# Nested Strassen products: a third one in the output projection, two in theta/phi, and an earlier sum in the last image

## The chip, the cores and the metric

The kernel runs on one core of a Trainium2 chip. The metric is the device time of one execution in microseconds (us); all times here are in that unit unless ns is written. The core has TensorE (matmuls, PE in the profile; its weight loads are PEld), VectorE (DVE), ScalarE (ACT), GpSimd (POOL) and SyncE (SP, which here issues most DMAs). They run their own instruction streams and meet at semaphores. Matmul results land in PSUM, everything else is in SBUF or, for what does not fit, in DRAM.

## The reference

The input x is 8 images of 512 channels and 1024 positions, in float32. For each image a self-attention layer with 8 heads of 64 channels is computed, and then a non-local block on its result:

```python
q, k, v = conv1x1(x, Wq, bq), conv1x1(x, Wk, bk), conv1x1(x, Wv, bv)
attn = softmax(einsum('bhdn,bhdm->bhnm', q, k) * scale)
out = einsum('bhnm,bhdm->bhdn', attn, v)
x1 = x + conv1x1(out, Wp, bp)                 # p

g, theta, phi = conv1x1(x1, g_w), conv1x1(x1, theta_w), conv1x1(x1, phi_w)   # 512 -> 256 channels, each with a bias
f = einsum('bcn,bdn->bcd', theta, phi) / n    # 256 x 256, no softmax
z = conv1x1(einsum('bcd,bdn->bcn', f, g), W_w, W_b) + x1
out = batch_norm(z over all images and positions) * gamma + beta
```

The batch norm needs all eight z, so the last step of the kernel goes over everything again.

## The kernel before, in words

**Images and stages.** The loop at the end of `unshifted` goes over the images b = 0 to 7. For each: attention of image b (scores L578, weighted sums L604), then q, v and k of image b + 1 (`six`), then p of image b (`project`, tile pp), theta and phi together (`theta_phi`, tile ptp, result tp), then `nonlocal_`: g (pg), f (pf), the product wf of f and W_w, and z (pz). In images 5 to 7 z is put off to the end (`late`). f of image 6 and the rest of its non-local block are computed in and after the last attention (`make_f`, two steps of scores after that attention's begin). In the last image p runs in a place of its own: the products of the attention's result o with the reciprocal denominators (`normalize`) run on DVE in four parts, two for each group of rows of o, and p comes right behind; in the images before it they run on GpSimd beside v.

**Seven products.** A projection is a product of a weight matrix with a data matrix. Both are cut into 2 x 2 blocks (quarters 11, 12, 21, 22) and multiplied with seven products in place of eight (Winograd's form of Strassen's scheme): `SEVEN` at L271 lists them with the weight block (0 to 6), the data block (11, 21, 22 or a difference t1 to t4), the PSUM slot and the quarters of the result that read the slot when the product is done. t1 = 12 − 11, t2 = 22 − t1, t3 = 22 − 12, t4 = 21 − t2 (`more_sums`). A slot is a double bank of PSUM; products that are listed with one slot add up in it, so the first matmul of the later one comes after DVE's reads of the earlier one. Weight blocks 3 to 6 are sums of the others (`weight_sums`); most are computed once, in image 0, and kept in DRAM (`keep`).

**Nested products.** A product of two blocks can itself be done with seven products of half the size. In q, k and v six of the seven are (L418, L421). In p of images 1 to 6, `FIVE` products are plain and products 1 and 2 are nested:

```python
FIVE = (SEVEN[0], SEVEN[1], SEVEN[2], SEVEN[3], ("s3t3", 5, "t3", 0, (("22", False), ("21", False))))
STEPS = [0] * 4 + [1] * 14
```

so the slots of the five run 0, 1, 0, 1, 0, and after the first four matmuls one inner matmul (a "step") follows each plain one, in slots of its own (`nested`, tiles pp_in_s at L299). Each step's PSUM result is read by DVE at once into a part of x (`first`, with the bias, or `add`). The inner products need the inner sums of their weight block (four 128 x 128 tiles that are kept beside the block, `extra`) and of their data block (`inner_sums`). Theta/phi is `SEVEN` with no nesting in every image.

**What sets the order.** Instructions given to `pe`, `dve` or `sp` keep the order of the program on their engine (`keep_in_program_order`); the others are placed by a scheduler between them. GpSimd runs, in the time of k, the sums t1 to t4 of o, the inner sums of its blocks 21 and t4, and additions into k.

**Weights.** `plan` lists the matrices in the order of use, `UNITS` into which loads each is cut. A unit goes into a ring of four buffers (`wr`), block 0 ("first") into one of two (`wf0`). `load_w()` issues the next unit on SyncE's queue, at fixed places of the program. A unit of two blocks has room for the inner sums behind each block. For theta/phi the two units are (3, 4, 2) and (6, 5, 1); for p they are (1, 2), (3, 4, 5) and (6). In the last image SyncE's queue also carries sixteen reloads of 512 KB (L918) between the loads of p's and theta/phi's weights, then the biases of theta and phi (L752), the second unit for theta/phi and WgT, and four reloads more (L925).

## Time and profile before

| | us |
|---|---|
| median of 3 runs | 2117.56 (2117.47 to 2119.9) |
| profiled execution | 2118.56 |
| its span | 2116.7 |
| TensorE busy | 2090.3 (99%) |
| VectorE busy | 1403.2 (66%) |
| ScalarE busy | 790.3 (37%) |
| GpSimd busy | 525.9 (25%) |
| p of image 1 (first to last matmul) | 515.44 to 538.65 |
| theta/phi of image 1 | 538.65 to 562.83 |
| p of the last image | 1980.28 to 2011.46 |

How to read it: the busy shares say which engine fills the span. The waits say what an engine stood still for: the total, how often, and the longest. The chain of waits follows the end of the execution back through whatever released each step; where an engine is never idle, the chain is that engine's own work. A timeline lists instructions in order with start and duration, and in brackets the idle time in front of them and what ended it. A matmul in float32 shows as two records; a plain one of p has 512 columns, an inner one 256. One of theta/phi has 256 columns, an inner one after the change 128.

### The profile page before, as it was taken

To read this page: it belongs to the slowest core of one execution; us is meant where nothing else is said; L and a number is where in the kernel's file an instruction comes from. 1 tells how busy PE (TensorE), PEld (TensorE's weight loads), DVE (VectorE), ACT (ScalarE), POOL (GpSimd) and SP (SyncE) were. 2 spreads that over 40 slices of the span, in tenths; PEclk is the share of its full clock that TensorE was granted. 3 is DMA by queue.
4 is the path that set the end of the run, shared out by engine and by line. 5 is a ranking of instruction groups with operands and counts; after the bars stand their busy time and mean duration, and the time that the engine had idled before them with its cause. 6 is when DMAs were issued, how large, how long until landed. Compare 5 with 4: busy or idle time off the path is not lost.

```text
span 2116.7 us, 33247 instructions
## 1 busy us (share of the span) xinstructions
PE 2090.3 (99%) x13486; PEld 1172.5 (55%) x13486; DVE 1403.2 (66%) x2051; ACT 790.3 (37%) x1045; POOL 525.9 (25%) x392
## 2 busy tenths in 40 slices
PE   9999999999999999999999999999999999999996
PEld 4535863357733677337763377633875348733362
DVE  5587567765578655786557766677565775567636
ACT  1464204642046410564106631166303653066016
POOL 0012900138001370014601155011640119011000
PEclk9999999999999999999999999999999999999998
DMA  6253533244232532425314253133544235222758
GB/s 229 83 148 76 174 147 111 40 92 141 100 117 40 120 110 98 120 40 141 122 62 125 40 152 121 72 101 41 170 139 140 39 63 169 75 31 40 268 188 319
DMA packets 71728, 243.56 MB, mean 115 GB/s; under 512 B 12688, under 2 KB 21136, under 8 KB 69520
## 3 DMA queue, kind: packets, MB, share of 16 engines
q1 hardware_dynamic: 60640, 215.01, 30.4%
q0 software_dynamic: 9072, 24.78, 9.5%
q8 instruction: 108, 1.77, 0.3%
q10 hardware_dynamic: 1856, 1.56, 0.3%
q14 instruction: 52, 0.43, 0.1%
HBM read 160.45 MB, written 47.32 MB: 98 GB/s over the span
## 4 chain that ended last, share of the span: by engine, by line
PE 97%; DVE 1%; ACT 1%; DMA 1%; issue 0%; SPq 0%; DVEq 0%
PE ps L578 21%; PE po L604 21%; PE ptp L342 9%; PE pp L342 7%; PE pv_in L418 6%; PE pq_in L421 6%; PE pk_in L421 6%; PE pg L342 4%; PE pz L342 3%; PE pf L801 2%; PE pp_in_s L299 2%; PE pq L388 1%; PE pq L342 1%; PE pv L385 1%; PE pv L342 1%; PE pk L388 1%
## 5 line engine op out<-in xcount | busy, mean ns | idle before, releaser
L581 ACT ACTIVATE e<-ps 128x1024 f32<-128x1024 f32 x512 | 523.0, 1025 | 422.9 <-PE ps L578 412.2
L587 DVE TENSOR_TENSOR acc<-acc,e 128x1024 f32<-128x1024 f32 x384 | 469.9, 1224 | 103.1 <-ACT e L581 92.9
L578 PE MATMUL ps<-q,k 64*64 64x512 f32 x4096 | 529.3, 589 | 0.0
L604 PE MATMUL po<-e,v 64*64 64x512 f32 x4096 | 528.6, 589 | 0.0
L617 POOL DMA_DIRECT2D fold<-acc x189 | 144.8, 766 | 1358.3 <-PE ps L578 690.6
L604 PEld LDWEIGHTS po<-e,v 64*64 64x64 f32 x4096 | 156.6, 133 | 282.9 <-issue 275.5
L578 PEld LDWEIGHTS ps<-q,k 64*64 64x64 f32 x4096 | 155.5, 133 | 283.5 <-issue 277.3
L844 ACT ACTIVATE g<-pg,gb 128x512 f32<-128x512 f32 x31 | 21.3, 688 | 447.0 <-PE pg L342 446.9
L585 DVE TENSOR_TENSOR acc<-e,e 128x1024 f32<-128x1024 f32 x64 | 78.3, 1224 | 121.2 <-ACT e L581 119.0
L342 PE MATMUL ptp<-w_tp,t_x 128*128 128x256 f32 x512 | 114.4, 379 | 0.0
L342 PE MATMUL pp<-t_o,w_WpT 128*128 128x512 f32 x208 | 103.4, 605 | 4.6 <-DVE t_o L252 4.6
L342 PEld LDWEIGHTS ptp<-w_tp,t_x 128*128 128x128 f32 x512 | 97.3, 190 | 13.2
L342 PE MATMUL ptp<-w_tp,x 128*128 128x256 f32 x384 | 86.8, 379 | 0.0
L342 PEld LDWEIGHTS ptp<-w_tp,x 128*128 128x128 f32 x384 | 73.0, 190 | 13.3 <-issue 3.8
L429 DVE TENSOR_TENSOR v<-v,pv_in 128x256 f32<-128x256 f32 x112 | 46.3, 421 | 43.8 <-PE pv_in L418 37.3
L429 DVE TENSOR_TENSOR k<-k,pk_in 128x256 f32<-128x256 f32 x112 | 46.8, 421 | 39.4 <-PE pk_in L421 35.0
L342 PE MATMUL pp<-o,w_WpT 128*128 128x512 f32 x144 | 67.7, 592 | 0.0
L427 ACT COPY v<-pv_in 128x256 f32<-128x256 f32 x84 | 31.4, 374 | 95.8 <-DVE T_pv L429 25.5
L427 ACT COPY k<-pk_in 128x256 f32<-128x256 f32 x84 | 31.3, 373 | 91.6 <-PE pk_in L421 89.9
L684 POOL TENSOR_TENSOR o<-o,r 128x1024 f32<-128x1024 f32 x28 | 65.3, 2372 | 0.0
L772 DVE TENSOR_TENSOR tp<-tp,ptp 128x1024 f32<-128x1024 f32 x24 | 29.3, 1221 | 51.2 <-PE ptp L342 51.2
L737 DVE SCALAR_TENSOR_TENSOR x<-pp,bp,x 128x512 f32<-128x512 f32 x52 | 37.6, 746 | 38.5 <-PE pp L342 38.5
(230 smaller groups left out, 2954.8 us busy)
## 6 DMA issues: line engine op xcount, KB each, us to landing
fold<-acc POOLq DMA_DIRECT2D x189, 128.0 KB, 3.1
w_WqT<-kept_WqT SPq DMA_DIRECT2D x21, 896.0 KB, 4.9
w_WvT<-kept_WvT SPq DMA_DIRECT2D x21, 896.0 KB, 5.0
w_WkT<-kept_WkT SPq DMA_DIRECT2D x21, 896.0 KB, 6.2
r<-den_d SPq DMA_DIRECT2D x32, 512.0 KB, 6.8
x<-in_x_dram SPq DMA_DIRECT2D x30, 512.0 KB, 5.9
spill<-x SPq DMA_DIRECT2D x24, 512.0 KB, 4.0
z<-spill SPq DMA_DIRECT2D x24, 512.0 KB, 9.9
```

The source lines that it names most:

```text
L342: pe(nc.tensor.matmul(to_ps, lhsT(k), rhs(k), start=(s, at) not in begun, stop=(k == nk - 1), skip_group_check=True))
L418: pe(nc.tensor.matmul(ps[:, i, :], d[:, i * P:(i + 1) * P], a, start=start and not i, stop=True, skip_group_check=True))
L421: pe(nc.tensor.matmul(ps, a, d, start=start, stop=True, skip_group_check=True))
L427: nc.scalar.copy(piece(q, i, j), ps)
L429: dve(nc.vector.tensor_tensor(piece(q, i, j), piece(q, i, j), ps, ALU.add))
L578: pe(nc.tensor.matmul(ps[c * P // 2:(c + 1) * P // 2, j, :], k[r, p, keys], q[r, p, h * 512:(h + 1) * 512], start=True, stop=True, skip_gr ...
L581: nc.scalar.activation(e, ps, AF.Exp, scale=SCALE)
L585: nc.vector.tensor_tensor(accs[u], es[u, 0], e, ALU.add)
L587: ins = nc.vector.tensor_tensor(accs[u], accs[u], e, ALU.add)
L604: pe(nc.tensor.matmul(ps[j * D:(j + 1) * D, r, :], v[keys, m, (2 * p + j) * D:(2 * p + j + 1) * D], e[keys, j, :], start=(m == 0), stop=(m ...
L617: nc.gpsimd.dma_start(to, part_of, accum_op=ALU.add)
L684: dve((engine or nc.vector).tensor_tensor(at, at, of, ALU.mult))
```

## The change

Four things are edited together.

- **p, images 1 to 6:** block 6 (quarter 22 of o) is nested as well. The list `FOUR` has the plain products 11, s1t1, s2t2 and s3t3 in slots 0, 1, 0, 0; s1t1 is now read for quarters 22 and 12, and s4 is gone from the list. Inner steps come two after each plain matmul from the fifth to the fourteenth, and one after the fifteenth. The inner sums of block 22 of o are added to GpSimd's work beside k. p's adds are pinned on DVE, and t1 and t2 of x1, the data of theta/phi, are now emitted around the add into quarter 22.
- **Theta/phi, images 1 to 7:** five plain products and two nested ones, 2 and then 1; the fourteen steps begin after the third plain product. t4 of x1 and the inner sums of t4 and of block 21 are on GpSimd. An inner result here has positions on the partitions, so one step is two matmuls of 128 columns. The sums of theta for f are emitted after the last plain product. All first reads and adds of theta/phi are pinned on DVE.
- **Weights:** theta/phi's units become (1, 2), (3, 4, 5), (6), so three loads in place of two; p's unit (6,) gets room for inner sums. In image 0 the inner sums of the newly nested weights are computed on DVE (`nest`) and kept; in this image the load of WgT is issued behind the keeping of p's blocks.
- **Last image:** t1 of o is emitted between the products of o for the first group of rows and those for the second, t2 behind the last one.

```diff
-             "WpT": ((1, 2), (3, 4, 5), (6,)), "tp": ((3, 4, 2), (6, 5, 1)),
+             "WpT": ((1, 2), (3, 4, 5), (6,)), "tp": ((1, 2), (3, 4, 5), (6,)),
...
+        def roomy(self, n):
+            return len(self.blocks(n)) == 2 or self.name == "WpT" and self.blocks(n) == (6,)
...
-    STEPS = [0] * 4 + [1] * 14
+    FOUR = (SEVEN[0], ("s1t1", 3, "t1", 1, (("22", True), ("12", True))), ("s2t2", 4, "t2", 0, (("12", False),)),
+            FIVE[4])
+
+    INNER = {"p": (FOUR, ((1, "21", "11", False), (2, "t4", "21", True), (6, "22", "12", False)),
+                   [0] * 4 + [2] * 10 + [1]),
+             "tp": (FIVE, ((2, "t4", "21", True), (1, "21", "11", False)), [0] * 24 + [1] * 14)}
...
+                if positions_out:
+                    ps = ps.rearrange("p (i f) -> p i f", f=P)
+                    for i in range(2):
+                        pe(nc.tensor.matmul(ps[:, i, :], d[di][:, i * P:(i + 1) * P], a[wi], start=start and not i,
+                                            stop=True, skip_group_check=True))
...
+        nest = 0 < b < B - 1
+        plain_add = add_to(xt, dve if nest else lambda ins: None)
+
+        def add(q, ps):
+            if nest and q == "22":
+                more_sums(x1, (1,), dve)
+            plain_add(q, ps)
+            if nest and q == "22":
+                more_sums(x1, (2,), dve)
...
+        def sums():
+            if "t3" not in data:
+                for i in (4,) if b else (3, 4):
+                    more_sums(data, (i,), dve, nc.gpsimd if b else None)
+            if b:
+                for of in ("t4", "21"):
+                    inner_sums(data, of, dve, nc.gpsimd)
+
+        def third_sum():
+            if "t3" not in data:
+                more_sums(data, (3,), dve)
...
-                more = [lambda of=of: inner_sums(nxt["o"], of, dve, nc.gpsimd) for of in ("21", "t4")]
+                more = [lambda of=of: inner_sums(nxt["o"], of, dve, nc.gpsimd) for of in ("21", "t4", "22")]
...
-            for one in normalize(nxt["d"]):
+            nxt["o"] = data_sums(quarters_of(o), f"o_{b}", ())
+            for n, one in enumerate(normalize(nxt["d"])):
                 one()
+                if n % 2:
+                    more_sums(nxt["o"], (n // 2 + 1,), dve)
+            between[1] = lambda: more_sums(nxt["o"], (3, 4), dve)
...
+        if b == 0:
+            between = {4: lambda: nest(w, 6)}
...
         if b == 0:
             w_p = w
+            kept["WpT"] = dict(kept["plain"])
+            keep("WpT", w_p, (2,))
...
-        between = {} if last else {5: lambda: b < B - 2 and of_theta.append(f_sums(b, tps[0], 0))}
+        between = {} if last else {4 if b else 5: lambda: b < B - 2 and of_theta.append(f_sums(b, tps[0], 0))}
...
         tp = theta_phi(b, w, data, tpb, between)
         if b == 0:
-            keep("tp", w)
-            kept["WpT"] = dict(kept["plain"])
             keep("WpT", w_p, (0,))
             load_w()
+            keep("tp", w, ("first", 1, 2))
+            for i in (1, 2):
+                nest(w, i)
+            keep("tp", w, (0,))
         load_w("first")
-        load_w(times=2)
+        load_w(times=3)
```

More of the change, by code (lines that the diff above doesn't have):

```diff
@@ L116, in unshifted @@
     PAIRS = ((1, 6), (3, 4), (5, 2))
-    UNITS = {"WqT": PAIRS, "WkT": PAIRS, "WvT": PAIRS, "WpT": ((1, 2), (3, 4, 5), (6,)), "tp": ((3, 4, 2), (6, 5, 1)),
+    UNITS = {"WqT": PAIRS, "WkT": PAIRS, "WvT": PAIRS, "WpT": ((1, 2), (3, 4, 5), (6,)), "tp": ((1, 2), (3, 4, 5), (6,)),
              "WgT": (range(7),)}
     WIDTH = 14 * P
-    INNER = (1, 2)
     class Weights:
@@ L131, in __getitem__, with blocks @@
             return self.at[at[1]][(slice(None), *at[2:])]
+        def blocks(self, n):
+            return (0,) if n == "first" else UNITS[self.name][n]
+        def roomy(self, n):
+            return len(self.blocks(n)) == 2 or self.name == "WpT" and self.blocks(n) == (6,)
         def place(self, n, t):
             size, to = 2 * self.half, 0
-            blocks = (0,) if n == "first" else UNITS[self.name][n]
+            blocks = self.blocks(n)
             for i in blocks:
@@ L138, in place @@
                 to += size
-                if n != "first" and len(blocks) == 2:
+                if self.roomy(n):
                     self.extra[i] = t[:, to:to + 3 * P].rearrange("p (i f) -> p i f", i=3)
@@ L146, in whole @@
             t = self.tiles[n]
-            if n == "first" or len(UNITS[self.name][n]) != 2:
+            if not self.roomy(n):
                 return t
-            return t.rearrange("p (b f) -> p b f", b=2)[:, :, :2 * self.half]
+            return t.rearrange("p (b f) -> p b f", b=len(self.blocks(n)))[:, :, :2 * self.half]
         def inner(self, i):
@@ L208, in inner_weights, with nest @@
                                      (s4, a12, s2, ALU.subtract))]
+    def nest(w, i):
+        for one in inner_weights(w, i):
+            one()
     def keep_inner(w):
@@ L282, in unshifted, with nested @@
     FIVE = (SEVEN[0], SEVEN[1], SEVEN[2], SEVEN[3], ("s3t3", 5, "t3", 0, (("22", False), ("21", False))))
-    STEPS = [0] * 4 + [1] * 14
-    def nested(name, w, data, tags, first, add):
+    FOUR = (SEVEN[0], ("s1t1", 3, "t1", 1, (("22", True), ("12", True))), ("s2t2", 4, "t2", 0, (("12", False),)),
[3 more added lines that the diff above has]
+             "tp": (FIVE, ((2, "t4", "21", True), (1, "21", "11", False)), [0] * 24 + [1] * 14)}
+    def nested(name, w, data, tags, first, add, goes_to, positions_out):
         slots = [bank(tag, f"{name}_in_{tag}") for tag in tags]
-        goes_to = {1: ("11", "21", False), 2: ("21", "t4", True)}
-        for n, (q, di, begins) in enumerate(goes_to[i] for i in INNER):
-            a, d = w.inner(INNER[n]), data[f"inner {di}"]
+        for n, (outer, of, q, begins) in enumerate(goes_to):
+            a, d = w.inner(outer), data[f"inner {of}"]
             pair = slots[::-1] if n % 2 else slots
@@ L298, in nested @@
                 ps = pair[s % 2 if s < 2 else 1][:, s // 2, n % 2 * 256:(n % 2 + 1) * 256]
-                pe(nc.tensor.matmul(ps, a[wi], d[di], start=s not in begun, stop=True, skip_group_check=True))
+                start = s not in begun
                 begun.add(s)
-                for to, is_first in reads:
-                    c = rows(q).start + int(to[0]) - 1
-                    at = cols(q).start + (int(to[1]) - 1) * 256
-                    (first if is_first and begins else add)((slice(c, c + 1), slice(at, at + 256)), ps)
+                if positions_out:
[3 more added lines that the diff above has]
+                                            stop=True, skip_group_check=True))
+                else:
+                    pe(nc.tensor.matmul(ps, a[wi], d[di], start=start, stop=True, skip_group_check=True))
+                for to, is_first in reads:
+                    i, j = int(to[0]) - 1, int(to[1]) - 1
+                    if positions_out:
+                        to = q, i, j
+                    else:
+                        c, at = rows(q).start + i, cols(q).start + j * 256
+                        to = slice(c, c + 1), slice(at, at + 256)
+                    (first if is_first and begins else add)(to, ps)
                 yield
     def seven(name, w, data, positions_out, first, add, between=None, early=False,
-              by_chunk=False, inner=False):
+              by_chunk=False, inner=None):
         nk, half = w.shape[2], w.shape[3]
@@ L315, in seven @@
         slots, begun = {}, set()
-        steps, counts = iter(()), iter(STEPS if inner else ())
+        steps, counts = iter(()), iter(())
         if inner:
             free[:] = [tags[1], tags[2], tags[3], tags[0]]
-            steps = nested(name, w, data, tags[2:], first, add)
+            products, goes_to, counts = INNER[inner]
+            counts = iter(counts)
+            steps = nested(name, w, data, tags[2:], first, add, goes_to, positions_out)
+        else:
+            products = LATER if early == "later" else EARLY if early else SEVEN
         def read(reads, ps):
@@ L323, in read @@
                 (first if is_first else add)(to, ps)
-        products = FIVE if inner else LATER if early == "later" else EARLY if early else SEVEN
         for n, (what, wi, di, s, reads) in enumerate(products):
@@ L728, in attention, with project @@
         return o["o"], all_denominators, normalize
-    def project(b, xt, o, w, between, data=None):
+    def project(b, xt, w, between, data, x1):
         def first(q, ps):
@@ L739, in first @@
                     dve(ins)
-        if not data:
-            data = data_sums(quarters_of(o), f"o_{b}", (1, 2), pin=dve)
-            between = {**between, 1: lambda: more_sums(data, (3, 4), dve)}
-        seven(f"pp_{b}", w, data, False, first, add_to(xt), between, early=b == B - 1 and "later", inner=0 < b < B - 1)
+        nest = 0 < b < B - 1
[6 more added lines that the diff above has]
+                more_sums(x1, (2,), dve)
+        seven(f"pp_{b}", w, data, False, first, add, between, early=b == B - 1 and "later", inner="p" if nest else None)
     tps = []
@@ L759, in at, with as_tp, add @@
         def at(q):
+            if isinstance(q, tuple):
+                q, i, j = q
+                m, c = (int(q[1]) - 1) * NB // 2 + j * NB // 4, (int(q[0]) - 1) * CI + i * P
+                return tp[:, m:m + NB // 4, c:c + P]
             return tp[:, (int(q[1]) - 1) * NB // 2:int(q[1]) * NB // 2, (int(q[0]) - 1) * CI:int(q[0]) * CI]
-        def as_tp(ps):
-            return ps.rearrange("p h (i f) -> p (h i) f", f=CI)
+        def as_tp(q, ps):
+            return ps if isinstance(q, tuple) else ps.rearrange("p h (i f) -> p (h i) f", f=CI)
         def first(q, ps):
-            ins = nc.vector.tensor_tensor(at(q), as_tp(ps), tpb[:, int(q[0]) - 1].to_broadcast([P, NB // 2, CI]),
-                                          ALU.add)
-            if q == "11":
-                dve(ins)
-        seven(f"ptp_{b}", w, data, True, first,
-              lambda q, ps: nc.vector.tensor_tensor(at(q), at(q), as_tp(ps), ALU.add),
-              {0: lambda: "t3" in data or more_sums(data, (3, 4), pin=dve), **between})
+            to, of = at(q), tpb[:, int((q[0] if isinstance(q, tuple) else q)[0]) - 1]
+            if isinstance(q, tuple):
+                of = of[:, :, q[1] * P:(q[1] + 1) * P]
+            ins = nc.vector.tensor_tensor(to, as_tp(q, ps), of.to_broadcast(list(to.shape)), ALU.add)
+            if q == "11" or b:
+                dve(ins)
+        def add(q, ps):
+            ins = nc.vector.tensor_tensor(at(q), at(q), as_tp(q, ps), ALU.add)
+            if b:
+                dve(ins)
+        def sums():
+            if "t3" not in data:
+                for i in (4,) if b else (3, 4):
+                    more_sums(data, (i,), dve, nc.gpsimd if b else None)
+            if b:
+                for of in ("t4", "21"):
[3 more added lines that the diff above has]
+                more_sums(data, (3,), dve)
+        seven(f"ptp_{b}", w, data, True, first, add, {0: sums, **({1: third_sum} if b else {}), **between}, inner="tp" if b else None)
         return tp
@@ L1087, in unshifted @@
         w = weights("WpT", sums_done=True)
-        project(b, xt, o, w, between, nxt.get("o"))
+        if b == 0:
+            between = {4: lambda: nest(w, 6)}
+        x1 = data_sums(quarters_of(xt), f"x1_{b}", ())
+        project(b, xt, w, between, nxt["o"], x1)
         if b == 0:
             w_p = w
+            kept["WpT"] = dict(kept["plain"])
+            keep("WpT", w_p, (2,))
         load_w("first")
@@ L1095, in unshifted @@
                 nc.sync.dma_start(spill[b][:, cc, :], xt[:, cc, :])
-        data = data_sums(quarters_of(xt), f"x1_{b}", (1, 2, 3, 4) if last else (1, 2))
+        data = x1
+        if last or not b:
+            more_sums(data, (1, 2, 3, 4) if last else (1, 2))
         if last:
@@ L1102, in unshifted @@
         w = weights("tp")
-        between = {} if last else {5: lambda: b < B - 2 and of_theta.append(f_sums(b, tps[0], 0))}
+        between = {} if last else {4 if b else 5: lambda: b < B - 2 and of_theta.append(f_sums(b, tps[0], 0))}
         if b == 0:
             weight_sums(w, corner["tp"], (3, 4, 5), dve)
-            def nest_p(i):
-                for one in inner_weights(w_p, i):
-                    one()
-            between.update({1: lambda: weight_sums(w, corner["tp"], (6,), dve), 2: lambda: nest_p(1), 3: lambda: nest_p(2)})
+            between.update({1: lambda: weight_sums(w, corner["tp"], (6,), dve), 2: lambda: nest(w_p, 1),
+                            3: lambda: nest(w_p, 2)})
         tp = theta_phi(b, w, data, tpb, between)
         if b == 0:
-            keep("tp", w)
-            kept["WpT"] = dict(kept["plain"])
             keep("WpT", w_p, (0,))
             load_w()
+            keep("tp", w, ("first", 1, 2))
+            for i in (1, 2):
+                nest(w, i)
+            keep("tp", w, (0,))
         load_w("first")
-        load_w(times=2)
+        load_w(times=3)
         def before_wf():
```

## The prediction

> **What bounds the kernel now.** I read the busy shares first, then TensorE's waits, then the chain of waits in one image, then the engines' timelines at the two places that the diff touches. All times are in us.

> ```profile
> PE 2090.3 (99%) x13486; PEld 1172.5 (55%) x13486; DVE 1403.2 (66%) x2051; ACT 790.3 (37%) x1045; POOL 525.9 (25%) x392
> ```
> TensorE is busy for the whole span, so a microsecond of matmul saved counts in full, and so does one of new waiting. DVE has a third of the span free, GpSimd three quarters.

> ```profile
> PE count L1152 <- DVE good L1150: 8.5, 1, 8.5
> PE pp L342 <- DVE t_o L252: 4.6, 1, 4.6
> ```
> TensorE waits twice in all for longer than 1.1: at the very end, and once in the last image's p. Nothing else can be won by removing a wait.

> ```profile
> 515.44 4.29 PE pp L342 x10
> 519.73 0.43 PE pp_in_s L299 x2
> 520.17 0.86 PE pp L342 x2
> ...
> 538.65 24.17 PE ptp L342 x112
> ```
> This is the chain in image 1, in start and duration (two records are one fp32 matmul). p runs 515.44 to 538.65: 20 plain matmuls of 0.858 and 14 inner ones of 0.432, 23.2, with no gap. tp is 7 products of 3.453.

> ```profile
> 729.80 3.45 PE pv L385 x16
> 733.26 18.76 PE pv_in L418 x168
> ```
> v shows the inner form that tp is to get: 168 records in 18.76 are 0.1117 each.

> ```profile
> 528.80 0.75 DVE L737 SCALAR_TENSOR_TENSOR x<-pp,bp,x 128x512 f32<-128x512 f32 x1 [0.44 <-PE pp L342]
> 529.47 0.48 DVE L737 SCALAR_TENSOR_TENSOR x<-pp_in_s,bp,x 128x256 f32<-128x256 f32 x1
> 533.10 0.42 DVE L448 TENSOR_TENSOR x<-x,pp_in_s 128x256 f32<-128x256 f32 x1 [0.81 <-PE pp_in_s L299]
> 533.96 1.22 DVE L448 TENSOR_TENSOR x<-x,pp 128x1024 f32<-128x1024 f32 x1 [0.44 <-PE pp L342]
> 538.69 2.35 DVE L448 TENSOR_TENSOR x<-x,pp 128x1024 f32<-128x1024 f32 x2 [1.23 <-PE pp L342]
> ```
> These are DVE's reads of PSUM in p: 0.42 for an inner result, 1.22 for a whole product, 0.75 (pitch 0.67) for each half of a first read. A read begins 0.04 after TensorE's end (538.65 to 538.69).

> ```profile
> 1980.28 3.60 PE L342 MATMUL pp<-o,w_WpT 128*128 128x512 f32 x8
> 1988.47 5.99 PE L342 MATMUL pp<-t_o,w_WpT 128*128 128x512 f32 x8 [4.59 <-DVE t_o L252]
> ```
> ```profile
> 1977.60 2.36 DVE L684 TENSOR_TENSOR o<-o,r 128x1024 f32<-128x1024 f32 x2 [3.29 <-DMA r<-den_d]
> 1984.92 2.36 DVE L684 TENSOR_TENSOR o<-o,r 128x1024 f32<-128x1024 f32 x2 [4.96 <-DMA r<-den_d]
> 1987.20 1.22 DVE L252 TENSOR_TENSOR t_o<-o 128x1024 f32<-128x1024 f32 x1
> ```
> In the last image p's second product needs t1, which stands behind four products of o, the last two waiting for a transfer. t1 itself needs only the first two, done by 1979.96.

> ```profile
> 1985.00:1990.00 5.00, 1.53 (x2) 0.83 (x3) 4.97 (x5) 0.00 (x0) 0.00 (x0) 0.63 1.02 394
> 1990.00:1995.00 5.00, 5.00 (x9) 2.05 (x8) 1.50 (x3) 0.00 (x0) 0.00 (x0) 0.69 1.02 404
> 1995.00:2000.00 5.00, 5.00 (x13) 2.22 (x12) 4.30 (x5) 0.00 (x0) 0.00 (x0) 1.00 1.03 415
> ```
> The three last columns are granted clock, DMA share and GB/s. That idle time also cost clock: 0.63 and 0.69, then 1.00. Six products after it took 2011.46 − 1988.47 = 22.99 instead of 6 × 3.434 = 20.60, so 2.4. And DMA is saturated here at about 410 GB/s by sixteen reloads of z.

> ```profile
> 2004.91 0.33 SPq L163 DMA_DIRECT2D w_tp<-kept_tp  x1
> ```
> ```profile
> w_tp<-kept_tp SPq DMA_DIRECT2D x1, 768.0 KB, 9.0
> ```
> SyncE issues the second unit of tp's weights behind those reloads at 2004.91, and it lands 9.0 later, at 2013.9.

> **The change, part by part** (the sum stands on the profiled execution of 2118.56, 1.0 above the median of 2117.56).

> *1. Third nested product in p, images 1 to 6.* A plain product of 4 × 0.858 = 3.43 becomes 7 × 0.432 = 3.02: −0.41 × 6 = **−2.5**. p without waits is then 22.8.

> *2. New waits in p, images 1 to 6.* Two of them.
> First, s3t3 accumulates in the slot that s2t2 just left. Before, s4 in the other slot and its inner steps lay between them (over 5 us). Now only inner steps 15 and 16 do (0.86), and DVE must read those two before the add of s2t2 into quarter 12, as the changed order has it. From the end of step 16: 0.04, its read 0.42, 0.03 because the add updates the same quarter (dependent DVE pairs at 302.33 and 303.05 stand 0.72 apart at 0.69 each), the add 1.22, and 0.05 until TensorE starts (1988.42 to 1988.47 above): 1.8. Bounds: with neither inner read ahead of it, 0.04 + 1.22 + 0.05 − 0.86 = 0.45; with one more first read of 0.75 in front, 2.55. I take 1.8, since every term is a row.
> Second, s1t1 is now read twice, for 22 and for 12: four half reads instead of two. From s1t1's end DVE does one (0.67), the inner reads of steps 7 and 8 (0.34, 0.40), three more (2.01), then step 9's (0.48), for which step 11 waits: 3.9 and about 0.1 of hand-over, while TensorE has 3.44 of work until then. 0.6; bounds 0 and 0.9.
> 2.4 × 6 = **+14.4** (0.45 × 6 = 2.7 to 3.45 × 6 = 20.7).

> [...]

> *3. tp's two nested products, images 1 to 7.* A plain one is 3.453, 28 records of 0.1117 are 3.13: −0.33 each, −0.65 an image; images 1 to 6 give **−3.9** (bound 0, if weight loading showed between shorter records; v's 168 show none). The cover: t4 and eight inner sums on GpSimd, one of 2.36 and eight of 0.73 by its rows at 498.38 and 507.77, start some 4.4 after p's end and give the first inner operand at about 7.5; it is needed 11.6 after p's end, after three plain products. If GpSimd took twice as long the spare 4 would be gone. DVE's inner reads (0.42 each, one per 0.87) fit beside the plain ones. Also at nothing: the inner sums of 22 of o (4 × 0.73) delay k's additions on GpSimd (513.50) by 2.9, read only in the next attention; t1 and t2 of x1 now stand around p's last adds on DVE, ready 1.7 and 3.3 after p's end against 3.5 and 6.9; theta's sums start after tp's end, so theta's and phi's (2 × 2.55) end about 7.7 after it, while f starts at 8.58 (562.83 to 571.41): 0.9 is left. SyncE's third load per image and 0.57 MB more of weights (1.4 at 410 GB/s) hide under DMA's mean of 115 GB/s.

> *4. Image 6.* make_f in the last attention follows two steps of scores (1.72) and reads tp after two whole adds by s3t3, now last: 0.04 + 1.14 + 1.25 + 0.1 = 2.53. **+0.8** (0 to 1.7).

> *5. Image 0.* WgT is now loaded only after the keeping of p's nested weights, so its sums no longer run inside p (275.89 to 280) but after theta's sums, tp's last read and among the nested sums of tp's weights on DVE: 0.38 + 1.22 + about 1.9 (five of the sums at 0.28 with their hand-overs, two of 0.42) put the operand of g's second product 3.6 after tp's end; it is wanted at 1.72. **+1.9** (0, if they went first, to 4 with all eight ahead and ww, loaded behind them, late as well). Keeping tp and p and SyncE's issues behind it delay the next weights, which are used only after f.

> *6. Last image.* t1 after the second product of o removes the wait, 4.75 from 1983.72 to 1988.47, and the 2.4 of clock: p ends at 2004.3. tp's "11" fills TensorE until 2007.75. Then s1t1 needs weight block 3. It was in tp's first unit; now (3, 4, 5) is the second, and the first, issued at 1978.81, holds (1, 2), needed last. By the row above it lands at 2013.9: a wait of 6.15, and then the clock again, 2.4. With tp's −0.65: −7.15 + 6.15 + 2.4 − 0.65 = **+0.8**. Bounds: with this queue's shortest nearby landing for such a block, 4.2 (median of w_tp elsewhere), the wait is 1.4 without a drop, −6.4; with 11.4 (gwf, the next transfers) +3.2. I take 9.0: same queue position, same load.

> What happens to the clock after a wait of 1.8 no row tells; after idles of up to 0.5 it stayed at 1.00, after 4.75 it fell. I take no drop. [...] Charging 2.4 for each wait in p instead would add 14.4.

> Sum: −2.5 + 14.4 − 3.9 + 0.8 + 1.9 + 0.8 = **+11.5**: 2130.1 against 2118.56, which is 2129.1 against the median.

> **The rivals.**
> *A, the slot wait in p is hidden (not slower).* For: DVE idles about half of each step there. Against: its reads are in a fixed order. Without part 2's +14.4 the time is 2114.7. It decides where p's waits fall under 2.4 − 11.5 / 6 = 0.5 an image.
> *B, tp's second unit lands in time* (before 2007.75). For: elsewhere 4.2. Against: the saturated queue. 6.15 + 2.4 less: 2120.5.
> *C, each 1.8 wait drops the clock too.* +14.4: 2143.5.
> *D, one more cover is gone:* GpSimd's sums late in tp, f's sums past f's start, or ww late in image 0. 0.3 to 1 in each of six images or 2 to 4 once: 2131 to 2136.

> **How the numbers follow.** Forecast 0.60, A 0.06, B 0.13, C 0.07, D 0.14. The range goes from B to just past D, 2120 to 2138, and leaves out A, C and some of B. A measurement tells 0.2% (4.2) from no change: 2113.3 to 2121.8 is the same. Faster needs A and B together: 0.04. Same is the rest of A and most of B that overlaps it: 0.12. Slower: 0.84.

> **What would show it.** Right: p in images 1 to 6 lasts about 25.2, with one wait of about 1.8 on DVE's add into x before s3t3 and one of 0.6 before an inner step; tp is 23.5; t_o is gone from TensorE's waits; in the last image tp's second product waits about 6 for w_tp and the granted clock falls after it; in image 0 pg waits about 2 for w_WgT. Wrong: p at 22.8 without gaps (A); w_tp landing before 2008 (B); a clock under 1.00 in p (C); a wait on GpSimd's inner sums in tp, or in front of f (D).

## The result and the profile after

The changed kernel takes 2134.64 us (median of 4 runs, 2133.56 to 2136.1) against 2117.51 for the kernel before: a ratio of 1.008, 95% interval 1.0062 to 1.0097. It is 17.1 slower; 11.5 were forecast (2129.1, range 2120 to 2138).

The page of the changed kernel, busy shares, then its list of TensorE's waits (total, number, longest):

```profile
PE 2088.8 (98%) x13690; PEld 1179.3 (55%) x13690; DVE 1447.8 (68%) x2190; ACT 790.5 (37%) x1045; POOL 601.9 (28%) x478
```
```profile
PE pp L369 <- DVE x L475: 10.6, 6, 1.8
PE count L1218 <- DVE good L1216: 8.6, 1, 8.6
PE ptp L369 <- DMA w_tp<-kept_tp: 6.9, 1, 6.9
PE pp_in_s L320 <- DVE x L764: 2.9, 6, 0.5
PE pg L369 <- DVE w_WgT L107: 1.9, 1, 1.9
PE warm_ps L498 <- DVE folds L513: 1.1, 1, 1.1
PE pq L369 <- DMA w_WqT<-in_WqT_dram: 0.7, 1, 0.7
PE pf L873 <- DVE tp L813: 0.7, 1, 0.7
```
TensorE works 1.5 less than before and waits in six places where it did not. The wait on t_o is gone. Five of the six were terms of the prediction; the sixth, 0.7 for w_WqT at the very start (8.4), is in no other profile here, so it is not put down to the change.

The chain of waits in p of image 1 shows both kinds of wait there:

```profile
528.30 0.87 PE pp L369 x2
529.20 0.75 DVE x L764
530.28 2.77 DVE x L764 x5
533.09 1.15 PE pp_in_s L320 x4
...
536.83 0.45 PE pp_in_s L320 x2
537.30 0.42 DVE x L475
537.73 0.43 DVE x L475
538.18 1.23 DVE x L475
539.46 1.12 PE pp L369 x2
```
From 529.20 the chain leaves TensorE for DVE's first reads of s1t1, and from 537.30 for two inner reads and then the add of s2t2 (538.18), after which s3t3 starts at 539.46: the second of them is the slot. Before, this stretch of the chain held TensorE alone. The pieces after each wait, 1.15 and 1.12, are longer than the 0.86 of four inner or two plain records elsewhere.

Where the time went, by the start of each stage on TensorE in the two profiled executions (2116.7 and 2134.3, so +17.6):

| stage | before | after | difference |
|---|---|---|---|
| g of image 0, up to f | 8.58 | 12.47 | +3.88 |
| p of images 1 to 6, each | 23.21 | 25.61 | +2.40 (× 6 = +14.4) |
| theta/phi of images 1 to 6, each (of image 6) | 24.17 (24.27) | 23.57 (23.66) | −0.60 (× 6 = −3.6) |
| first scores of image 7, up to f | 1.88 | 2.60 | +0.73 |
| p of image 7 | 31.18 | 24.03 | −7.14 |
| theta/phi of image 7 | 24.17 | 33.38 | +9.21 |

These make +17.5. Windows of the changed kernel (granted clock, DMA share and GB/s last) show the clock in the last image after its wait for block 3:

```profile
2023.00:2031.00 8.00, 1.10 (x5) 0.64 (x4) 3.17 (x3) 0.00 (x0) 5.57 (x8) 0.66 1.03 407
2031.00:2034.00 3.00, 3.00 (x9) 2.37 (x8) 0.00 (x0) 0.00 (x0) 0.00 (x0) 0.50 1.02 408
2034.00:2037.00 3.00, 3.00 (x11) 2.51 (x10) 0.19 (x1) 0.00 (x0) 0.00 (x0) 0.70 1.02 404
2037.00:2040.00 3.00, 3.00 (x15) 2.64 (x15) 1.04 (x1) 0.00 (x0) 0.00 (x0) 1.00 0.27 100
```

And they show a lower clock in image 0, after a wait of only 1.95:

```profile
304.50:307.00 2.50, 1.91 (x5) 0.57 (x4) 2.46 (x6) 0.42 (x1) 0.00 (x0) 1.00 0.00 0
307.00:309.00 2.00, 0.64 (x1) 0.30 (x2) 1.97 (x9) 0.27 (x1) 0.00 (x0) 0.92 0.00 0
309.00:311.00 2.00, 2.00 (x4) 0.94 (x3) 1.97 (x5) 0.00 (x0) 0.00 (x0) 0.50 0.46 186
```

### The profile page after: what moved, and what is told of

Same layout as the page of the kernel before. It is cut to its first block, busy times and chain, and to the rows that moved or that the text cites. A ratio compares the mean times of both kernels' runs of the same rounds, so it can differ in the third digit from the quotient of the medians.

```text
span 2134.3 us, 34029 instructions
## 1 busy us (share of the span) xinstructions
PE 2088.8 (98%) x13690; PEld 1179.3 (55%) x13690; DVE 1447.8 (68%) x2190; ACT 790.5 (37%) x1045; POOL 601.9 (28%) x478
## 4 chain that ended last, share of the span: by engine, by line
PE 93%; DVE 3%; DMA 3%; ACT 1%; issue 0%; ACTq 0%; SPq 0%; DVEq 0%
PE po L631 21%; PE ps L605 21%; PE ptp L369 7%; PE pv_in L445 6%; PE pq_in L448 6%; PE pk_in L448 6%; PE pp L369 5%; PE pg L369 4%; PE pz L369 3%; PE ptp_in_s L317 2%; PE pp_in_s L320 2%; PE pf L857 2%; PE pq L415 1%; PE pwf L912 1%; PE pv L369 1%; PE pv L412 1%
## 5 line engine op out<-in xcount | busy, mean ns | idle before, releaser
L369 PE MATMUL ptp<-w_tp,t_x 128*128 128x256 f32 x400 | 98.8, 388 | 6.9 <-DMA w_tp<-kept_tp 6.9
L369 PEld LDWEIGHTS ptp<-w_tp,t_x 128*128 128x128 f32 x400 | 74.1, 195 | 15.8 <-issue 7.3
L475 DVE TENSOR_TENSOR x<-x,pp_in_s 128x256 f32<-128x256 f32 x102 | 42.7, 420 | 43.7 <-PE pp_in_s L320 42.1
L369 PE MATMUL ptp<-w_tp,x 128*128 128x256 f32 x272 | 69.6, 380 | 0.0
L445 PE MATMUL pv_in<-w_WvT,i_t_x 128*128 128x128 f32 x448 | 59.2, 275 | 0.0
L369 PEld LDWEIGHTS pp<-t_o,w_WpT 128*128 128x128 f32 x208 | 39.0, 190 | 34.3 <-issue 18.2
L448 PE MATMUL pk_in<-i_t_x,w_WkT 128*128 128x256 f32 x224 | 57.8, 381 | 0.0
```

What stands on the lines that cost most here:

```text
L369: pe(nc.tensor.matmul(to_ps, lhsT(k), rhs(k), start=(s, at) not in begun, stop=(k == nk - 1), skip_group_check=True))
L445: pe(nc.tensor.matmul(ps[:, i, :], d[:, i * P:(i + 1) * P], a, start=start and not i, stop=True, skip_group_check=True))
L448: pe(nc.tensor.matmul(ps, a, d, start=start, stop=True, skip_group_check=True))
```

## The experiments

My theory: the waits in p come from when PSUM slots are read, those in images 0 and 7 from weights that are loaded late. Rivals: the third nested product overloads DVE; the pinned order does the harm; the clock falls on its own. The runs were made on several chips. The kernel before took 2117.84 beside the runs with reads by halves, two nested products, other units and WgT early, and 2116.68 beside those with the other queue, t1 alone and all of it mended; the changed kernel's 2134.64 stands beside 2117.51. Differences against it are therefore uncertain by about 1; the times of single stages, from the profiles, say more.

**Reads by halves in p.** The third nested product stays.

```diff
+            by_halves = inner == "p" and what in ("s1t1", "s2t2")
...
+                if by_halves and what == "s2t2" and k == nk - 1:
+                    half_reads(reads, ps, at)[0]()
+                else:
+                    if by_halves and i == len(work) - 1:
+                        later += half_reads(reads, ps, 0) + half_reads(reads, ps, 1)
+                    if later:
+                        later.pop(0)()
...
-                if b == B - 1 and q in ("11", "22"):
+                if nest or b == B - 1 and q in ("11", "22"):
```

> The changed kernel with its three nested products in p as they are, but the results of s1t1 and s2t2 are read by DVE in halves: s2t2's first half as soon as its first bank is done, s1t1's four halves one at a time between the later inner steps. Theory (the waits in p come from when a slot is read, not from the third nested product): both waits of each p go, with the 0.27 that TensorE takes longer after each; p lasts 16 x 0.858 + 21 x 0.432 = 22.8 instead of 25.61, six times -2.8, so about 2117.8. Rival (DVE cannot keep up with 21 inner reads and the rest): the wait moves to an inner step, p stays at 25 or more, 2131 or above.

Measured: 2119.59 (2118.97 to 2121.32), 15.1 less than the changed kernel. Neither wait of p is left in the list. But p is 23.17, not 22.8. The chain of this kernel says where the rest is:

```profile
530.30 0.86 PE pp L376 x2
531.16 0.86 PE pp_in_s L320 x4
532.03 1.04 PE pp L376 x2
...
534.79 0.86 PE pp_in_s L320 x4
535.65 1.04 PE pp L376 x2
```
Two plain matmuls, each the first behind a half read of its own slot, take 1.04 instead of 0.86. The half reads start at 531.20 and 534.83, 0.20 after the start of the inner step that follows their matmul (531.00, 534.63): the records of that matmul run to 531.16 and 534.79 (1.02 from 530.14 and 533.77), 0.16 into that step. So each read, 0.69 long, ends late, the matmul behind it starts 0.08 late (531.94 and 535.57 for 531.86 and 535.49), and its two records take 1.12 instead of 1.02, the other 0.10. The theory holds; DVE, with more and shorter reads in p, keeps up.

**Two nested products in p**, as before; the rest of the change stays.

```diff
-    INNER = {"p": (FOUR, ((1, "21", "11", False), (2, "t4", "21", True), (6, "22", "12", False)),
-                   [0] * 4 + [2] * 10 + [1]),
+    INNER = {"p": (FIVE, ((1, "21", "11", False), (2, "t4", "21", True)), [0] * 4 + [1] * 14),
```

> The changed kernel with p as before (five plain products, two nested, one inner step per matmul); all the rest stays changed. Theory: p of images 1 to 6 is 23.21 again, six times -2.40, about 2120.2, and no wait is left in p. Rival (p is longer because of t1 and t2 of x1 on DVE or the pinned adds): p stays over 24 and the time over 2125.

Measured: 2119.48 (2118.32 to 2120.79), p 23.21 in each of images 1 to 6, no wait in it. So t1 and t2 of x1 on DVE and the pinned adds cost p nothing; the +2.40 is the third product's alone. In this run and the one before it a new wait of 0.7 to 0.8 for ww appeared in image 0. There g up to f took 10.77, against 12.47 in the changed kernel, whose slower g had covered it.

**Other units for theta/phi.**

```diff
-"tp": ((1, 2), (3, 4, 5), (6,)),
+"tp": ((3, 4, 6), (1, 2), (5,)),
```

> The changed kernel with theta/phi's weights cut into (3, 4, 6), (1, 2), (5,), so that the unit loaded ahead of the reloads holds what the second to fourth products need. Theory (the last image waits for block 3 behind the reloads, and the clock falls after it): theta/phi of the last image takes 23.6 to 24 instead of 33.4, so -9.5 and about 2125. Rival 1 (the clock loss is there without that wait): -6.9 only, about 2127.7. Rival 2 (the next unit, blocks 1 and 2, is now what comes late): a wait of some us in front of the first inner step, 2127 to 2133.

Measured: 2128.69 (2127.63 to 2129.13), −6.0. Neither rival, and not the whole theory: theta/phi of the last image takes 27.44, because the next transfer is late. TensorE's and DVE's timelines:

```profile
2027.71 5.41 PE L369 MATMUL ptp<-w_tp,t_x 128*128 128x256 f32 x16 [1.91 <-DVE tp L808]
```
```profile
2026.43 2.36 DVE L808 TENSOR_TENSOR tp<-ptp,tpb 128x1024 f32<-128x1024 f32 x2 [2.65 <-DMA tpb<-in_theta_b_dram]
```
The first read of theta/phi adds the bias tpb, which SyncE also issues behind the sixteen reloads. s2t2 needs the slot of that read. With block 3 late, this did not show. The wait of 1.91 cost clock as well (0.87 from 2025 to 2030, 0.64 from 2030 to 2033, then 1.00): 27.44 − 23.57 = 3.87 in all.

**Biases and weights of the last image on another queue**, with those units.

```diff
-            sp(nc.sync.dma_start(t[:, k, 0, :], a[n].partition_broadcast(P)))
+            sp((nc.scalar if b == B - 1 else nc.sync).dma_start(t[:, k, 0, :], a[n].partition_broadcast(P)))
...
-        load_w(times=3 if b else 2)
+        load_w(times=3 if b else 2, dma=nc.scalar if last else None)
...
-        nc.sync.dma_start(ww, a["WwT"].rearrange("(c p) f -> p c f", p=P))
+        (nc.sync if b else nc.scalar).dma_start(ww, a["WwT"].rearrange("(c p) f -> p c f", p=P))
```

> The changed kernel with theta/phi's units (3, 4, 6), (1, 2), (5,) and, in the last image, the biases of theta and phi and the weights behind them issued on ScalarE's DMA queue instead of SyncE's, so not behind the sixteen reloads (ww of image 0 as well). Theory (with block 3 there, the first read of theta/phi waited for its bias, and TensorE for that read): theta/phi of the last image takes 23.6 with no wait, -9.8 against the changed kernel, about 2124.8. Rival (DMA itself is the limit, whoever issues): the bias lands about 8 after its issue all the same, and the wait of 1.9 stays, 2128.

Measured: 2124.52 (2123.96 to 2126.1), −10.1; theta/phi 23.57, −9.81, no wait. ScalarE's queue issued the weights here (times and durations of issues):

```profile
1990.57 0.36 ACTq L787 DMA_DIRECT2D tpb<-in_theta_b_dram  x1
1990.97 0.71 ACTq L787 DMA_DIRECT2D tpb<-in_phi_b_dram  x1
2011.24 3.77 ACTq L168 DMA_DIRECT2D w_tp<-kept_tp  x2
```
SyncE issued the biases at 2018.74 and the weights at 2021.30 in the changed kernel, 22.9 and 25.4 after the start of the last image's p (1995.86); here p starts at 1993.38, the biases go out 2.8 before it and the weights 17.9 after it, so 25.7 and 7.6 earlier. The transfers themselves still take long, 7.7 for blocks 1 and 2: what helped was the place in the queue. Biases and weights were moved together, so the run does not say what the weights alone were worth. p, with these transfers beside it, was 0.49 longer; what holds it there is not shown.

**t1 alone**, in the kernel before.

```diff
-            for one in normalize(nxt["d"]):
+            nxt["o"] = data_sums(quarters_of(o), f"o_{b}", ())
+            for n, one in enumerate(normalize(nxt["d"])):
                 one()
+                if n % 2:
+                    more_sums(nxt["o"], (n // 2 + 1,), dve)
+            between[1] = lambda: more_sums(nxt["o"], (3, 4), dve)
```

> The kernel before with nothing changed but the last image: t1 of o between the products for the two groups of rows, t2 after the last. Theory (the wait of 4.6 and the clock after it go, and with the old units nothing else comes late: the second unit, landing about 2014, is wanted at 2004.3 + 10.4): -7.1, about 2110.4. Rival (the transfers move too, or the unit is late by its landing of 9): -5 to -6, 2112.

Measured: 2112.91 (2112.42 to 2115.35) against 2116.68, a ratio of 0.9983 (0.9973 to 0.9992): −3.8, less than theory (−7.1) and rival (−5 to −6) had. p of the last image is 7.14 shorter, and 1.90 of it goes again in theta/phi, which waits for the bias as in the run with other units:

```profile
2012.41 3.72 PE L342 MATMUL ptp<-w_tp,t_x 128*128 128x256 f32 x16 [1.63 <-DVE tp L766]
```
The weights, which I had thought of, came in time; the bias did not. That leaves 5.2 in the profiles, whose spans differ by 5.9 (2116.7 and 2110.8). The profiled execution of the kernel before (2118.56) is 1.9 above the median here, which is most of the gap to 3.8; where the shorter ones save time no trace shows.

**WgT early in image 0.**

```diff
+                            3: lambda: (nest(w_p, 2), keep("WpT", w_p, (0,)), load_w()),
+                            5: lambda: (wgs.append(weights("WgT", pin=dve)), of_theta.append(f_sums(b, tps[0], 0)))})
...
         if b == 0:
-            keep("WpT", w_p, (0,))
-            load_w()
```

> The changed kernel with, in image 0 alone, WgT loaded as soon as p's nested weights are kept (inside theta/phi) and its sums done before theta's sums. Theory (the wait of 1.95 costs itself and then a spell of half clock): both go, 3.9 less, about 2130.8, and the granted clock stays at 1.00 in g of image 0. Rival (the clock falls there for another reason): 1.95 less, about 2132.7, with a clock under 1.00 left in g.

Measured: 2134.39 (2133.9 to 2135.24), no difference that can be told from the changed kernel. g up to f is 8.58 again, −3.88, as the theory has it. But then:

```profile
324.97 3.24 PE L912 MATMUL pwf<-ww,f 128*128 128x512 f32 x7 [2.24 <-DVE tg L925]
```
The wait is put down to DVE's tg, but in the changed kernel this product starts (326.75) before the first tg (327.72). SyncE issued ww at 315.24, behind three loads of 896 KB, and it took 9.6 to land, at about 324.9; in four other runs the profile puts a wait here, of 0.67 to 0.93, down to ww itself. In the profile 2.3 of the 3.9 come back there.

**Which wait costs clock?** Image 0's wait of 1.95 did in the changed kernel's profile and in that with other units, but g up to f was 10.77 and not 12.47 in those with reads by halves, with two nested products and with the other queue, after the same 1.95. So I lengthened the wait before s3t3: by a copy of another length in each image, and then with n = 512 and with n = 1024 in all six.

```diff
+            if nest and q == "12":
+                x1["t1"] = block(f"t1_{x1['name']}")
+                n = {1: 128, 2: 256, 3: 512, 4: 1024, 5: 2048, 6: 0}[b]
...
+                    dve(nc.vector.tensor_copy(i[:, :m], xt.rearrange("p a n -> p (a n)")[:, :m]))
             plain_add(q, ps)
```

> The changed kernel with an extra copy on DVE ahead of the add of s2t2 in p, longer from image to image (128, 256, 512, 1024 and 2048 columns in images 1 to 5, none in image 6): the wait before s3t3 grows from 1.77 to about 1.85, 1.95, 2.2, 2.9 and 4.1. The question is which wait costs clock, after 1.95 in image 0 did so in two of four profiles. If it is a chance that grows with the wait: p stays at 25.61 plus the copy in images 1, 2 and 6, and is about 2 longer still in 4 and 5, with a granted clock of 0.5 for some us. [...] If the clock does not fall in p at all: every p is 25.61 plus the copy.

> As the ladder, with the copy of 512 columns in all six images, so six waits of 1.98, where one of 1.98 cost clock before and one of 1.85 did not. If length alone decides: all six p are 27.5 (25.61 + 0.21 + 1.70). If it also depends on when the wait falls, as three of six waits of 1.95 in image 0 suggest: some of the six are 27.5 and some 25.8.

> As the ladder, with the copy of 1024 columns in all six images, so six waits of 2.38. If length alone decides: all six p are 27.9 (25.61 + 0.60 + 1.70). If it also depends on when the wait falls: some are 26.2, but fewer than with 1.98.

Measured: 2142.18, 2141.66 and 2142.92 (one execution each). p by image from the timelines; a p that is 1.70 longer than 25.61 plus its copy is marked *:

| wait before s3t3 in images 1 to 6 | p |
|---|---|
| 1.78, 1.84, 1.98, 2.38, 3.10, 1.77 (ladder) | 25.62, 25.69, 27.52*, 27.91*, 28.64*, 25.61 |
| 1.98 in all | 27.51*, 27.51*, 25.82, 27.52*, 25.82, 25.82 |
| 2.37 or 2.38 in all | 26.22, 27.91*, 26.21, 27.91*, 27.91*, 26.22 |

The windows of the run with 1.98 in all, images 1 and 3, both from just before the wait:

```profile
534.00:538.00 4.00, 2.88 (x11) 1.71 (x9) 2.42 (x6) 0.00 (x0) 0.00 (x0) 1.00 0.43 129
538.00:542.00 4.00, 3.15 (x7) 2.04 (x8) 1.22 (x2) 0.00 (x0) 0.00 (x0) 0.69 0.16 68
542.00:546.00 4.00, 4.00 (x13) 2.37 (x12) 1.68 (x4) 0.00 (x0) 0.00 (x0) 0.89 0.01 4
1058.00:1062.00 4.00, 2.95 (x11) 1.71 (x9) 2.33 (x6) 0.00 (x0) 0.00 (x0) 1.00 0.42 126
1062.00:1066.00 4.00, 3.07 (x10) 1.98 (x11) 1.72 (x3) 0.00 (x0) 0.00 (x0) 1.00 0.17 71
```
The same wait in the same place: the clock fell to 0.69 and 0.89 in one and stayed at 1.00 in the other. Length alone does not decide.

The traces' records of the granted clock show what went with each fall. In each of the twelve profiles (before, after and the ten runs), from the first rise of the clock on to the fall in the wait for `count`, the clock changes only at times that are whole multiples of 3.413 apart (to 0.004; its half-clock spells last 6.83 before, 3.41 and 10.24 after), and how these times lie against the kernel differs from execution to execution. So each trace can be cut into windows of 3.413, and TensorE's listed idle summed in each. Of the windows at full clock, 35 hold 1.91 or more of idle, and the clock is at half in the window behind 33 of them; 7324 hold 1.89 or less, and it falls behind none of these, so in these profiles it never fell on its own. (The two exceptions, with 1.95 and 2.01, are both in the run with 2.37.) A half clock stayed behind every window with idle left in it (0.68 the least) and ended behind the first without. For the waits above:

| wait | largest part in one window, clock fell | clock stayed |
|---|---|---|
| 1.95 in image 0 | 1.95, 1.95, 1.95 | 1.95, 1.79, 1.43, 1.24, 1.01 |
| 1.98 in p | 1.98, 1.98, 1.98, 1.97 | 1.58, 1.35, 1.19 |
| 2.37 or 2.38 in p | 2.38, 2.38, 2.38, 2.21 | 1.89, 1.81, 1.50 |

In the windows shown, image 1's wait (536.88 to 538.85) lies within one window, 536.09 to 539.51; image 3's is cut by an edge at 1061.75 into 0.79 and 1.19. This was read off the traces afterwards; no run was made to test it.

**All of it mended**: the third nested product with s1t1 and s2t2 taken in turns by halves, so that no matmul follows the read of its own slot; WgT early; the other units and queues.

```diff
+                (c, ps1, reads1), d2 = s1t1, work
+                work = [c[0], c[1], d2[0], d2[1], c[2], d2[2], d2[3], c[3]]
+                one = {m: half_reads(reads1, ps1, m) for m in range(2)}
+                when = {1: one[0][0], 2: one[0][1], 3: half_reads(reads, ps, 0)[0], 6: half_reads(reads, ps, 1)[0],
+                        7: one[1][0]}
```

> The changed kernel with all of it mended: in p, s1t1 and s2t2 are taken in turns by halves and read by halves, so that no product follows the read of its own slot (the 0.18 that was left twice in each p with reads by halves goes too); WgT early in image 0 and ww on ScalarE's queue; the last image as in the run with its weights and biases on ScalarE's queue. Theory: p 22.8 (-2.8 x 6), g of image 0 -3.9, the last image -9.8, so 2134.6 - 30.5 = about 2104. Rivals: GpSimd or DVE sums come late once TensorE no longer waits (2108 to 2112); p stays at 23.2 because the third nested product gains nothing (2106.5).

Measured: 2104.93 (2104.55 to 2105.6) against 2116.68, a ratio of 0.9945 (0.9931 to 0.9958): 11.8 faster than the kernel before and 29.7 faster than the changed one. All the waits of TensorE that are listed:

```profile
PE count L1240 <- DVE good L1238: 8.6, 1, 8.6
PE warm_ps L521 <- DVE folds L536: 1.1, 1, 1.1
PE pf L896 <- DVE tp L836: 0.7, 1, 0.7
PE den L694 <- ACT got L247: 0.3, 1, 0.3
```
p is 22.80 in images 1 to 6 (−0.41 against before, as the count of matmuls gave it), theta/phi 23.57. GpSimd's sums are nowhere waited for.

## Why the prediction was right, and where it was off

The direction and every place were right, and the time lay in the range; the size was 5.6 short. By the prediction's parts, in the profiled executions (one of each kernel):

1. *Third product, −2.5:* right. The mended kernel has −0.41 in each p.
2. *Waits in p, +14.4:* right in mechanism (reads by halves took them away, two nested products too), too small: 25.61 − 22.80 = 2.81 an image, so +16.9. The terms that were mis-sized are the two hand-overs. TensorE's listed idle was 1.77 and 0.49, near the 1.8 and 0.6 forecast, but the list ends a matmul with its record, which lasts 592 ns where the next one starts after 429 when it waits for nothing, so 0.16 later; and the first record after a wait, 533 ns to the next, takes another 0.10. Together 0.26 a wait, and 0.02 more on an inner record soon after the wait of 0.49.
3. *Nesting in theta/phi, −3.9:* −3.6. The covers held, GpSimd's among them.
4. *Image 6, +0.8:* +0.73.
5. *Image 0, +1.9:* +3.9. The wait was 1.95, as forecast. The step that failed is "no drop" of the clock for waits of about 2, which I took with no row behind it: here it fell in this execution, for the other 1.9 (1.7 of clock, the rest the hand-over). That it fell in the profiled execution is chance, since it did in three of eight with this wait. ww, which rival D names, was not late in the changed kernel, but was as soon as g was quicker.
6. *Last image, +0.8:* +2.07. −7.14 for −7.15; theta/phi's wait was 6.90 for 6.15, because the late unit was issued 25.4 after p's start and not 24.6 as in the kernel before (the reloads ahead of it took 21.2 to issue, not 19.85), and clock and hand-over cost 2.9 instead of 2.4 (33.38 − 23.57 − 6.90).

The missing 6.1 (17.6 for 11.5) is thus 2.5 in p, 2.0 in image 0, 1.3 in the last image and 0.3 in theta/phi.

Of the rivals, A (p's wait hidden) fell, and what it would have taken is now known: the reads by halves. B fell, with a landing of 9.0 once more. C was wrong for p (no drop in any p of the changed kernel) and right in kind for image 0. D came only when other waits went.

That s3t3 stands behind s2t2 in one slot, which part 2 charged with 1.8 an image, did cost that wait (1.77): with the third nested product in place, reads by halves brought p from 25.61 to 23.17, and taking s1t1 and s2t2 in turns besides brought it to 22.80.

## What to carry to other kernels

When a product is taken out of a sequence that alternates two accumulators, look at which two now stand side by side: the read between them, which cost nothing before, was a wait of 1.77 in each p here. Reading each half as it was done, and computing something else meanwhile, gave the product's gain back (p 22.80, against 23.21 before the change). And when a stage is made to start earlier, go through everything else that it reads, the small transfers (a bias) too, and ask where in which queue each was issued: in both images where a late load was mended, the next one in the queue was late.
